# A four-layer graph network on one core: list packing placed beside layer 1, rows and weights loaded at other points, early groups of layer 3 taken feature by feature

## The chip, the core and the metric

The kernel runs on one core of a Trainium2 chip. The engines named below are TensorE (PE, with its weight loads as PEld), VectorE (DVE), ScalarE (ACT), GpSimd (POOL) and SyncE (SP), which only issues DMAs. The metric is the device time of one execution in microseconds (us), less being better. The kernel before takes 2413.58 us, the median of three runs.

## The reference, cut to what matters

The input is `x` with 2708 rows of 512 features and a 0/1 adjacency matrix `adj` of 2708 x 2708 (symmetric, about 16 neighbours a row), all in float32. Four layers follow each other, each of the form `x = layernorm(x + layer(x))`:

```python
deg = maximum((adj != 0).sum(-1), 1)
# layer 0: relu((((adj + I) / deg[:, None]) @ x + x) @ W + b)
# layer 1: (dis[:, None] * adj * dis[None, :]) @ x @ W.T + b,   dis = deg**-0.5
# layer 2: two attention layers, each
proj = x @ W                       # 512 x 1024
Wh, Ws = split(proj, 2)
a = softmax(Wh @ Ws.T) * adj       # the softmax is over all 2708 columns
x = leaky_relu(a @ Wh + x)
# layer 3: adj @ (x @ W) + b
```

## The kernel before, in words

**Tiles.** Rows come in 22 blocks of 128, columns in six chunks (`CH`: four of 512, then 384 and 276), row blocks in six groups (`GROUPS`: 4, 4, 4, 4, 3, 3). Most tiles in SBUF are pages (128 x 512 float32) of one pool of 82; the 8 banks of PSUM are two halves of four. Every engine's instructions run in the order in which the program issues them: the class `Ordered` chains each one to the one before it on its engine. That helper is line 70, and so every instruction of the profile has line 70; the names of the tiles tell them apart.

**Layers 0, 1 and 3** (`Fast.step`) go chunk by chunk, and in a chunk group by group. `multiply` adds `x` (as a high and a low part, `xh` and `xl`) times the mask columns `m` to four accumulators `acc`, one for each 128 features. After the last group of a chunk `evict` copies them to `ht`; the product with the weights (`mm`), the residual and the layernorm of the chunk (`ends`) follow during the groups of the next chunk, with `run.phase` counting them.

**Lists.** An attention layer needs of each row only its neighbours. `index(k)`, a generator, works out for chunk `k` of layer 1 where each row's neighbours stand. It alternates DVE steps (`up`, `keep`, `place`, `at_row`, `hit`, `both`, `sums`) with PE steps (`rank`, `rest`, `list`); the result is `givers`. `work(engine)` runs the next step of the oldest list if it is that engine's. Before, `step` calls it for PE in phases 1 and 5 and for DVE when the phase becomes 4 and 6; what is left over runs inside the attention, called by `beat` in the projections and score loop, and `packed(k - 1)` forces what is due.

**Attention** (`Attention.layer`) takes a chunk of columns at a time. For block `j` of 22, PE forms scores `sp`, ACT copies them to `s`, and DVE keeps the greatest (`top`). PE transposes the greatest (`tr_top`, `tr_mx`). While the next chunk's scores run, `soften` takes the exponents of this chunk's (`s<-s`, DVE and ACT), sums them, multiplies by the mask, and SP stores them into a table `pairs` in DRAM, beside the rows of `Wh`. After a chunk's last store POOL gathers from it (`g`, indirect DMAs by `givers`, at most 10 ahead), and `weigh` multiplies what was gathered into `acc`. `end` adds the row of x (`xr`) and, in the second layer, the layer's input (`x1`); both are loaded on SP's queue when a block's first `weigh` is issued. `advance`, `later` and `until` are a planner's clock by estimated costs, which sets when `weigh` and `end` are called.

**Ends of the attention layers.** In the last chunk the generator `fill` gives PE other work. For the first attention layer it is `second`: it loads `wt`, `w` and `xt`, mixes the second layer's weights (`mix`) and projects. For the second layer it is `early`: it runs the first four row groups of layer 3 for the first three chunks (`TWO`), so that part of layer 3 lies beside the end of the attention; after group 3 of a chunk, ACT copies its four accumulators to pages `begun`, and `evict` adds them later. The first `next(fill)`, which issues the loads, comes once, after the 14th of the 22 score blocks of the last chunk:

```python
if n == 13 and k + 1 == len(chunks):
    next(fill)
```

Of the kernel before, what the change touches and what calls it, by code (L numbers as in the profile page):

```python
# [24 lines left out]
DC = D // P  # L25
BANK = 512

CH = [(0, 512), (512, 512), (1024, 512), (1536, 512), (2048, 384), (2432, 276)]

GROUPS = [(0, 4), (4, 8), (8, 12), (12, 16), (16, 19), (19, 22)]  # L30
# [442 lines left out]
def blocks_of(k):  # L473

    c0, cw = CH[k]
    return [(c0 // P + q, q * P, min(P, cw - q * P)) for q in range(-(-cw // P))]
# [10 lines left out]
def cost(columns):  # L487

    return 4 * columns / 2400
# [24 lines left out]
class Fast:  # L514
# [83 lines left out]
    def early(self, run):  # L598

        seq = run.seq  # L600
        self.load(*seq[0])
        self.load(*seq[1])
        yield True
        self.prepare(*seq[0])
        for t in range(4 * TWO):
            ly, k, g = seq[t]
            if t < 2:
                self.attention.need(GROUPS[t + 2][1] - 1)
            self.load(*seq[t + 2])
            if t == 4:  # L610
                self.load_weights(ly)
            if t == 4 * TWO - 1:
                self.attention.need(GROUPS[4][1] - 1)
                for j in range(*GROUPS[4]):
                    ly.rows[j] = self.attention.made[j]
            self.prepare(*seq[t + 1])
            for j in range(*GROUPS[g]):
                self.multiply(ly, k, g, [j])
                self.attention.advance(2 * cost(CH[k][1]))
                yield True  # L620
            if g == 3:
                ly.begun[k] = [self.page(f"begun{k}_{d}") for d in range(DC)]
                for d, t in enumerate(ly.begun[k]):
                    self.nc.scalar.copy(t[:, : CH[k][1]], ly.acc[k][d][:, : CH[k][1]])


    def layernorm(self, rows):
# [72 lines left out]
    def load_rows(self, ly, j):  # L700
        if ly.rows[j] is None:
            ly.rows[j] = self.page(f"x{ly.number}_{j}")
            self.nc.gpsimd.dma_start(ly.rows[j], ly.source[j])

    def halve(self, ly, j):

# [103 lines left out]
            self.k.masks[k][:, b0 : b0 + len(ats), :], at_b[:, : len(ats), :cw]  # L810
        )

    def multiply(self, ly, k, g, only=None):
        nc, cw = self.nc, CH[k][1]
        blocks = only or range(*GROUPS[g])
        two = ly.number == 3 and k < TWO
        starts, stops = ((0, 16), (15, NB - 1)) if two else ((0,), (NB - 1,))
        if blocks[0] in starts:

            half = 0 if two and blocks[0] == 0 else k  # L820
            ly.acc[k] = [self.bank(half, f"acc{ly.number}_{k}_{d}") for d in range(DC)]
        ms = ly.done["m", k, g]
        todo = [(d, j) for d in range(DC) for j in blocks]
        if k == 0 and g + 1 < len(GROUPS):
            todo.sort(key=lambda a: a[1])
        for d, j in todo:
            for x, first in ((ly.hi, True), (ly.lo, False)):
                nc.tensor.matmul(
                    ly.acc[k][d][:, :cw],
                    x[j][:, bass.ts(d, P)],  # L830
                    ms[j - GROUPS[g][0]][:, :cw],
                    start=(j in starts and first),
                    stop=(j in stops and not first),
                )
# [158 lines left out]
    def step(self, run, t):  # L993

        ly, k, g = run.seq[t]
        self.other = (k + 1) % 2
        self.before_products(run, t)
        if ly.number == 0 and (k, g) == (1, 0):
            self.attention.blank()
        if ly.number == 1 and k == len(CH) - 1 and g in (2, 3, 4):  # L1000
            self.attention.begin(g - 2)
        self.multiply(ly, k, g)
        if run.before and run.phase in (1, 5):
            self.work("PE")
        if run.before:
            self.ends(run, run.phase)
            run.phase += 1
            if run.phase in (4, 6):
                self.work("DVE")
        if g == (4 if ly.number == 3 and k < TWO else 3):  # L1010
            self.residual(ly, k)
            if k == len(CH) - 1 and ly is not run.layers[-1]:
                self.load_weights(run.layers[1])
        if g == len(GROUPS) - 1:
            if ly.number == 3:
                self.biased(ly, k)
            if ly.number == 0:
                self.degrees(ly, k, g)
            while run.before and run.phase < 2:
                self.ends(run, run.phase)  # L1020
                run.phase += 1
            self.evict(ly, k)
            run.before, run.phase = (ly, k), 0
            if ly.number == 1:
                self.jobs.append((k, self.index(k)))

    def ends(self, run, g):

# [173 lines left out]
class Chunk:  # L1202


    def __init__(self, ly, k):
        self.ly, self.k, self.cw = ly, k, CH[k][1]
        self.name = f"{ly.number}_{k}"
        self.blocks = blocks_of(k)
        self.s, self.masks, self.ends = {}, {}, []
        self.softened = 0  # L1210
        self.fetched, self.rden = [], None

        self.to_weigh = []
        for q, (i, _, _) in enumerate(self.blocks):
            ts = lists_of(i)
            self.to_weigh += [(q, t, t is ts[0], t is ts[-1]) for t in ts]
        self.to_fetch = [(q, t) for q, ts, _, _ in self.to_weigh for t in ts]
        self.first_fetch = self.to_fetch[0]
# [8 lines left out]
class Attention:  # L1227
# [93 lines left out]

    def project(self, ly, k):
        for _ in self.project_steps(ly, k):
            pass

    def project_steps(self, ly, k):

# [186 lines left out]
    def fetch(self, ch):  # L1514


        q, t = ch.to_fetch.pop(0)
        g = self.f.wide(f"g{ch.name}_{q}_{t}")
        i = ch.blocks[q][0]
        self.nc.gpsimd.indirect_dma_start(  # L1520
            out=g,
            out_offset=None,
            in_=ch.ly.pairs[ch.k % 2].rearrange("r j d -> (r j) d"),
            in_offset=bass.IndirectOffsetOnAxis(ap=self.k.givers[:, i, t : t + 1], axis=0),
            element_offset=(q // 2) * NP * (D + 2 * P) + (q % 2) * P,
        )

        begin = max(self.fetch_free, self.clock + (16 if (q, t) == ch.first_fetch else 0))
        self.fetch_free = begin + 1.15
        ch.fetched.append((g, self.fetch_free + 6))  # L1530
# [20 lines left out]
    def weigh(self, wait=False):  # L1551

        nc = self.nc
        self.fetch_ahead()
        ch = next((c for c in self.chunks if c.to_weigh), None)
        if ch is None:
            return False
        q, ts, first, last = ch.to_weigh[0]
        if len(ch.fetched) < len(ts):
            return False  # L1560
        if ch.fetched[len(ts) - 1][1] > self.clock and not wait:
            return False
        ch.to_weigh.pop(0)
        if ch.rden is None:
            self.divisor(ch)
        i, _, w = ch.blocks[q]
        gs = [ch.fetched.pop(0)[0] for _ in ts]
        if first:
            ch.acc = self.bank(1, f"acc{ch.name}_{q}")
            ch.x = self.page(f"xr{ch.name}_{q}")  # L1570
            given = self.k.saved[1] if ch.ly.number == 0 else self.k.between
            nc.sync.dma_start(ch.x[:w], given[i][:w])
            if ch.ly.number == 1:
                ch.first = self.page(f"x1{ch.name}_{q}")
                nc.sync.dma_start(ch.first[:w], self.k.saved[1][i][:w])
        c = (q % 2) * D
        for h, g in enumerate(gs):
            lo, m = (0, w) if len(gs) == 1 else (h * QW, QW)
            nc.tensor.matmul(
                ch.acc[lo : lo + m],  # L1580
                g[:, c + lo : c + lo + m],
                g[:, P - (q % 2) * P : P - (q % 2) * P + D],
                start=first,
                stop=last,
            )
        self.advance(cost(D) if len(gs) == 1 else 1.1)
        if last:
            before = getattr(ch, "first", None)
            self.later(1.5, lambda a=(ch, q, ch.acc, ch.x, before): self.end(*a))
        self.fetch_ahead()  # L1590
        return True

# [45 lines left out]
    def layer(self, ly, chunks, fill):  # L1638
        f = self.f
        self.chunks, self.made = chunks, {}  # L1640
        for k, ch in enumerate(chunks):
# [3 lines left out]
            for n, j in enumerate(js):  # L1645
# [12 lines left out]
                    f.packed(k - 1)  # L1658
                if n == 4 and k + 1 < len(chunks):
                    self.load_moving(chunks[k + 1])  # L1660
                if n == 13 and k + 1 == len(chunks):
                    next(fill)
                if old and n == 0:
                    self.greatest(old, js[-1])
# [43 lines left out]
    def second(self, first):  # L1708

        ly = self.layers[1]  # L1710
        mixing = self.mix(1)
        next(mixing)
        self.load_w(ly)
        self.load_xt(ly, 0)
        yield True
        yield from mixing
# [73 lines left out]
```

## Time and profile before

| | |
|---|---|
| three runs | 2408.57 to 2414.01 us, median 2413.58 us |
| the profiled execution | 2413.0 us, its span 2411.3 us |
| mean granted TensorE clock | 0.982 |
| layer 0, 0 to 360 us | PE busy 342.8, DVE 319.9 |
| layer 1, 360 to 618 | PE 257.9, DVE 158.9 |
| first attention projections, 618 to 781 | PE 161.6, DVE 66.8 |
| scores, first attention layer, 781 to 1296 | PE 494.1, DVE 377.4 |
| mix and projections, 1296 to 1527 | PE 218.5, DVE 57.5 |
| scores, second attention layer, 1527 to 2027 | PE 487.7, DVE 341.7 |
| end of attention with early layer 3, 2027 to 2190 | PE 139.6, DVE 71.0 |
| rest of layer 3, 2190 to 2411 | PE 203.5, DVE 82.0 |

The stages overlap at their edges; the times are cut where most of the work changes. A stage's length less PE's busy time is what PE idles there. A busy PE may also run at half clock, which shows in the granted clock. The lines of the profile give, for a group of instructions, the engine, the operation, the tile written and the tiles read (`out<-in`), and in brackets the idle time before it with the engine and tile that ended it.

### The profile page before, as it was taken

What the parts mean: (1) busy time and instruction counts of PE and PEld (TensorE: products, weight loads), DVE (VectorE), ACT (ScalarE), POOL (GpSimd) and SP (SyncE); (2) the same over time, 40 slices, a digit from 0 to 9 for tenths busy, and PEclk for the clock granted to TensorE, in tenths of its full rate; (3) what the DMA queues carried; (4) which work ended last, traced back from release to release, by engine and by line L of the source; (5) the groups of instructions that cost most, each with busy time, mean ns of one, the idle gap of its engine ahead of it and who ended that gap; (6) DMA issues with size and microseconds to landing.
All of it is one profiled execution on the core that took longest, in us unless ns stands there. A gap on an engine that the chain in (4) does not pass through costs nothing.

```text
span 2411.3 us, 26147 instructions
## 1 busy us (share of the span) xinstructions
PE 2305.6 (96%) x8518; PEld 1322.7 (55%) x8518; DVE 1475.1 (61%) x2842; ACT 653.8 (27%) x1300; POOL 770.3 (32%) x895
## 2 busy tenths in 40 slices
PE   8999999999999998999998999999999998899997
PEld 6677777777545443443554444444443454566685
DVE  7989984756535688757665511247868785623513
ACT  6444352321110122222222210123223233421121
POOL 6545541111000001634556450001643657451000
PEclk9999999999999999999999999999999998899999
DMA  9755552223454114868889895314967889872311
GB/s 349 253 182 165 175 174 77 77 75 110 150 189 181 47 53 126 297 224 284 269 292 353 269 387 207 130 40 154 325 215 270 307 273 345 247 251 93 115 54 41
DMA packets 311126, 471.74 MB, mean 196 GB/s; under 512 B 59874, under 2 KB 189418, under 8 KB 310980
## 3 DMA queue, kind: packets, MB, share of 16 engines
q1 hardware_dynamic: 249684, 236.61, 29.9%
q0 software_dynamic: 61296, 233.37, 28.0%
q8 instruction: 69, 1.13, 0.2%
q14 instruction: 77, 0.63, 0.1%
HBM read 316.01 MB, written 153.85 MB: 195 GB/s over the span
## 4 chain that ended last, share of the span: by engine, by line
PE 80%; DVE 10%; issue 3%; DMA 3%; ACT 1%; POOL 1%; SPq 1%; another core or an unknown queue 1%; DVEq 0%; ACTq 0%; POOLq 0%
PE acc L70 30%; PE sp L70 26%; PE mm L70 9%; PE wst L70 6%; PE z L70 6%; DVE s L70 2%; DVE sum L70 1%; SPq L70 1%; DMA pairs<-s 1%; DVE top L70 1%; DMA at<-in_adj_t 1%; DVE at_row L70 1%; DMA xt<-t 1%; DVE st L70 1%
## 5 line engine op out<-in xcount | busy, mean ns | idle before, releaser
L70 POOL DMA_INDIRECT g<-pairs,givers x510 | 516.3, 1012 | 955.5 <-issue 624.5
L70 PE MATMUL sp<-xs,wst_sb 128*128 128x512 f32 (+3 forms) x2112 | 805.2, 547 | 0.0
L70 PE MATMUL acc<-m,xh 128*128 128x512 f32 (+2 forms) x1584 | 588.7, 378 | 27.5 <-ACT begun L70 14.0
L70 PEld LDWEIGHTS sp<-xs,wst_sb 128*128 128x128 f32 (+1 forms) x2112 | 382.1, 187 | 403.4 <-issue 338.3
L70 PE MATMUL acc<-m,xl 128*128 128x512 f32 (+2 forms) x1584 | 574.5, 368 | 4.1 <-DVE xl L70 3.3
L70 PEld LDWEIGHTS acc<-m,xh 128*128 128x128 f32 x1584 | 301.7, 190 | 89.2 <-ACT begun L70 16.1
L70 PEld LDWEIGHTS acc<-m,xl 128*128 128x128 f32 x1584 | 302.2, 191 | 52.4 <-issue 6.2
L70 PE MATMUL acc<-g 128*32 128x512 f32 (+1 forms) x1020 | 265.2, 610 | 10.0 <-DMA g<-pairs,givers 7.9
L70 ACT COPY s<-sp 128x512 f32<-128x512 f32 (+2 forms) x252 | 132.8, 529 | 469.2 <-PE sp L70 311.2
L70 DVE TENSOR_TENSOR top<-top,s 128x512 f32<-128x512 f32 (+5 forms) x240 | 149.5, 623 | 161.2 <-ACT s L70 112.4
L70 PE MATMUL mm<-w,ht 128*128 128x512 f32 (+1 forms) x528 | 226.1, 600 | 7.7 <-DVE ht L70 7.7
L70 ACT ACTIVATE s<-s 128x512 f32<-128x512 f32 (+3 forms) x264 | 150.4, 580 | 294.4 <-DVE s L70 204.7
L70 ACT CAST m<-at 128x512 fp32r<-128x512 uint8 (+5 forms) x396 | 199.1, 567 | 68.0 <-DMA at<-mask 42.3
L70 DVE TENSOR_TENSOR sum<-sum,s 128x512 f32<-128x512 f32 (+4 forms) x252 | 156.8, 622 | 39.4 <-issue 20.9
L70 DVE TENSOR_TENSOR s<-s,a 128x512 f32<-128x512 f32 (+3 forms) x264 | 165.9, 628 | 9.1
L70 DVE TENSOR_TENSOR s<-s,shift 128x512 f32<-128x512 f32 (+3 forms) x264 | 162.8, 620 | 10.3 <-ACT shift L70 10.3
L70 PEld LDWEIGHTS mm<-w,ht 128*128 128x128 f32 (+1 forms) x528 | 96.9, 188 | 126.6 <-issue 112.3
L70 PEld LDWEIGHTS acc<-g 128*32 128x32 f32 (+1 forms) x1020 | 77.1, 136 | 147.4 <-issue 125.0
L70 PE MATMUL wst<-xt,mixed 128*128 128x512 f32 (+2 forms) x384 | 150.5, 545 | 1.7 <-issue 1.7
L70 PE MATMUL z<-w,xt 128*128 128x512 f32 (+1 forms) x352 | 150.2, 595 | 0.0
L70 DVE COPY z_sb<-z 128x512 f32<-128x512 f32 (+1 forms) x44 | 30.3, 690 | 175.8 <-PE z L70 130.8
L70 POOL DMA_DIRECT2D x<-o x44 | 25.9, 595 | 349.8 <-DVE o L70 346.1
(159 smaller groups left out, 1662.0 us busy)
## 6 DMA issues: line engine op xcount, KB each, us to landing
pairs<-s SPq DMA_DIRECT2D x378, 128.0 KB
pairs<-z_sb SPq DMA_DIRECT2D x84, 512.0 KB
at<-in_adj_t SPq DMA_DIRECT2D x88, 256.0 KB
xres<-x POOLq DMA_DIRECT2D x44, 256.0 KB
x<-o POOLq DMA_DIRECT2D x43, 256.0 KB
x<-x POOLq DMA_DIRECT2D x35, 256.0 KB
at<-mask SPq DMA_DIRECT2D x32, 256.0 KB
xt<-t SPq DMA_DIRECT2D x32, 256.0 KB
```

What stands on the lines that cost most here:

```text
L70: ins = call(*args, **kw)
```

## The change

Four things are done, and they touch separate places.

1. **List packing.** In layer 1, PE steps are taken in phases 1, 3, 4 and 5, and DVE steps when the phase becomes 3, 4 and 5, and right after a chunk's last group, when its list is appended. The first two attention projections call `beat` too.
2. **Rows of x.** `fetch` issues the load of `xr` (and `x1`) with a block's first gather; `weigh` no longer does.
3. **Loads at the attention's ends.** `fill` is advanced after the 6th, 12th and 20th score block of the last chunk. For the first attention layer these are `wt`, then `w`, then `xt`; for the second layer nothing, then masks and rows of x for layer 3, then the preparation (`xh`, `xl`, `m`) of the first group. Layer 3's rows go to SP's queue.
4. **Early groups.** From the second early group on, `multiply` is called with one feature at a time over the group's blocks, where it took one block at a time over the features; in group 3 the copy to `begun` follows each feature.

```diff
@@ -598,10 +598,12 @@
         seq = run.seq
+        yield True
         self.load(*seq[0])
         self.load(*seq[1])
         yield True
         self.prepare(*seq[0])
+        yield True
         for t in range(4 * TWO):
             ly, k, g = seq[t]
@@ -614,14 +616,19 @@
                     ly.rows[j] = self.attention.made[j]
             self.prepare(*seq[t + 1])
-            for j in range(*GROUPS[g]):
-                self.multiply(ly, k, g, [j])
+            if g == 3:
+                ly.begun[k] = []
+            for n, j in enumerate(range(*GROUPS[g])):
+                if t == 0:
+                    self.multiply(ly, k, g, [j])
+                else:
+                    self.multiply(ly, k, g, ds=[n])
                 self.attention.advance(2 * cost(CH[k][1]))
+                if g == 3:
+                    b = self.page(f"begun{k}_{n}")
+                    self.nc.scalar.copy(b[:, : CH[k][1]], ly.acc[k][n][:, : CH[k][1]])
+                    ly.begun[k].append(b)
                 yield True
-            if g == 3:
-                ly.begun[k] = [self.page(f"begun{k}_{d}") for d in range(DC)]
-                for d, t in enumerate(ly.begun[k]):
-                    self.nc.scalar.copy(t[:, : CH[k][1]], ly.acc[k][d][:, : CH[k][1]])
@@ -700,7 +707,8 @@
         if ly.rows[j] is None:
             ly.rows[j] = self.page(f"x{ly.number}_{j}")
-            self.nc.gpsimd.dma_start(ly.rows[j], ly.source[j])
+            queue = self.nc.sync if ly.number == 3 else self.nc.gpsimd
+            queue.dma_start(ly.rows[j], ly.source[j])
     def halve(self, ly, j):
@@ -810,17 +818,17 @@
         )
-    def multiply(self, ly, k, g, only=None):
+    def multiply(self, ly, k, g, only=None, ds=range(DC)):
         nc, cw = self.nc, CH[k][1]
         blocks = only or range(*GROUPS[g])
         two = ly.number == 3 and k < TWO
         starts, stops = ((0, 16), (15, NB - 1)) if two else ((0,), (NB - 1,))
-        if blocks[0] in starts:
+        if blocks[0] in starts and 0 in ds:
             half = 0 if two and blocks[0] == 0 else k
             ly.acc[k] = [self.bank(half, f"acc{ly.number}_{k}_{d}") for d in range(DC)]
         ms = ly.done["m", k, g]
-        todo = [(d, j) for d in range(DC) for j in blocks]
+        todo = [(d, j) for d in ds for j in blocks]
         if k == 0 and g + 1 < len(GROUPS):
             todo.sort(key=lambda a: a[1])
@@ -1000,12 +1008,12 @@
             self.attention.begin(g - 2)
         self.multiply(ly, k, g)
-        if run.before and run.phase in (1, 5):
+        if run.before and run.phase in (1, 3, 4, 5):
             self.work("PE")
         if run.before:
             self.ends(run, run.phase)
             run.phase += 1
-            if run.phase in (4, 6):
+            if run.phase in (3, 4, 5):
                 self.work("DVE")
         if g == (4 if ly.number == 3 and k < TWO else 3):
@@ -1023,6 +1031,7 @@
             if ly.number == 1:
                 self.jobs.append((k, self.index(k)))
+                self.work("DVE")
     def ends(self, run, g):
@@ -1209,6 +1218,7 @@
         self.softened = 0
         self.fetched, self.rden = [], None
+        self.x, self.first = {}, {}
         self.to_weigh = []
@@ -1321,7 +1331,7 @@
     def project(self, ly, k):
         for _ in self.project_steps(ly, k):
-            pass
+            self.f.beat()
     def project_steps(self, ly, k):
@@ -1516,7 +1526,14 @@
         q, t = ch.to_fetch.pop(0)
         g = self.f.wide(f"g{ch.name}_{q}_{t}")
-        i = ch.blocks[q][0]
+        i, _, w = ch.blocks[q]
+        if q not in ch.x:
+            ch.x[q] = self.page(f"xr{ch.name}_{q}")
+            given = self.k.saved[1] if ch.ly.number == 0 else self.k.between
+            self.nc.sync.dma_start(ch.x[q][:w], given[i][:w])
+            if ch.ly.number == 1:
+                ch.first[q] = self.page(f"x1{ch.name}_{q}")
+                self.nc.sync.dma_start(ch.first[q][:w], self.k.saved[1][i][:w])
         self.nc.gpsimd.indirect_dma_start(
             out=g,
@@ -1563,16 +1580,10 @@
         if ch.rden is None:
             self.divisor(ch)
-        i, _, w = ch.blocks[q]
+        w = ch.blocks[q][2]
         gs = [ch.fetched.pop(0)[0] for _ in ts]
         if first:
             ch.acc = self.bank(1, f"acc{ch.name}_{q}")
-            ch.x = self.page(f"xr{ch.name}_{q}")
-            given = self.k.saved[1] if ch.ly.number == 0 else self.k.between
-            nc.sync.dma_start(ch.x[:w], given[i][:w])
-            if ch.ly.number == 1:
-                ch.first = self.page(f"x1{ch.name}_{q}")
-                nc.sync.dma_start(ch.first[:w], self.k.saved[1][i][:w])
         c = (q % 2) * D
         for h, g in enumerate(gs):
@@ -1585,8 +1596,8 @@
         self.advance(cost(D) if len(gs) == 1 else 1.1)
         if last:
-            before = getattr(ch, "first", None)
-            self.later(1.5, lambda a=(ch, q, ch.acc, ch.x, before): self.end(*a))
+            a = (ch, q, ch.acc, ch.x.pop(q), ch.first.pop(q, None))
+            self.later(1.5, lambda: self.end(*a))
         self.fetch_ahead()
         return True
@@ -1658,7 +1669,7 @@
                 if n == 4 and k + 1 < len(chunks):
                     self.load_moving(chunks[k + 1])
-                if n == 13 and k + 1 == len(chunks):
+                if n in (5, 11, 19) and k + 1 == len(chunks):
                     next(fill)
                 if old and n == 0:
@@ -1710,7 +1721,9 @@
         mixing = self.mix(1)
         next(mixing)
+        yield True
         self.load_w(ly)
+        yield True
         self.load_xt(ly, 0)
         yield True
```

## The prediction

> **What bounds the kernel now.** I read the page first, then TensorE's waits, then windows of the stages around the waits, and last the timelines of the engines that release them. The page:
>
> ```profile
> PE 2305.6 (96%) x8518; PEld 1322.7 (55%) x8518; DVE 1475.1 (61%) x2842; ACT 653.8 (27%) x1300; POOL 770.3 (32%) x895
> ```
>
> TensorE sets the time. The change removes no matmul, so it can gain only what TensorE idles, plus the half clock after idling. Its waits, with total, times and longest in us:
>
> ```profile
> PE acc L70 <- ACT begun L70: 14.0, 3, 6.6
> PE list L70 <- DVE both L70: 11.5, 4, 7.3
> PE tr_top L70 <- DVE top L70: 8.9, 1, 8.9
> PE acc L70 <- ACT m L70: 8.6, 5, 3.7
> PE acc L70 <- DMA g<-pairs,givers: 7.9, 2, 6.4
> ```
>
> Their places are in the TensorE timeline (start, length, operation, idle time before it; two more begun waits, 3.25 and 4.11, stand before 2139.88 and 2190.46):
>
> ```profile
> 930.65 0.74 PE L70 MATMUL list<-both,at_row 128*128 128x24 bf16 x22 [7.35 <-DVE both L70]
> ...
> 1322.89 0.88 PE L70 MATMUL tr_top<-ident,top 128*128 128x128 f32 x3 [8.89 <-DVE top L70]
> ...
> 2014.57 3.67 PE L70 MATMUL acc<-g 128*128 128x512 f32 x4 [6.44 <-DMA g<-pairs,givers]
> ...
> 2090.29 0.80 PE L70 MATMUL acc<-m,xh 128*128 128x512 f32 x1 [6.60 <-ACT begun L70]
> ```
>
> Windows (length; busy us of PE, PEld, DVE, ACT, POOL; granted clock; DMA share; GB/s) show the cover in layer 1, its lack in the scores, a restart at half clock, and a full DMA:
>
> ```profile
> 420.00:480.00 60.00, 60.00 (x266) 44.14 (x265) 40.26 (x76) 17.45 (x35) 6.61 (x12) 1.00 0.24 78
> ...
> 900.00:960.00 60.00, 49.82 (x174) 22.57 (x173) 55.65 (x109) 16.25 (x29) 7.20 (x7) 0.91 0.36 112
> ...
> 2090.00:2096.00 6.00, 5.71 (x13) 4.48 (x14) 3.30 (x9) 4.39 (x10) 1.41 (x2) 0.50 1.03 345
> ```
>
> Work at clock c costs (1 - c) of its busy time: 2.9 us in the last row.
>
> **Packing moved beside layer 1.** In the scores DVE is busy 55.65 of 60 us, and a list step is a wait for TensorE:
>
> ```profile
> 926.36 3.22 DVE L70 TENSOR_TENSOR at_row<-upto,row 128x1024 bf16<-128x1024 bf16 x3
> ...
> 930.17 0.43 DVE L70 TENSOR_TENSOR both<-hit,block 128x264 bf16<-128x264 bf16 x1
> ```
>
> With hit (0.42) and the first half of both (0.29) between them that is 4.4 us a step, 6.7 where the place arithmetic precedes it (924.0 to 930.6). By the program order all packing now ends in the second attention projection, ahead of all scores. Six waits go: 1.36 (742.9), 2.59 (796.2), 1.88 (896.9), 2.63 (909.5), 7.35 (922.7), and 1.57 for mx at 963.8, where DVE was late: 17.4. The half clock after two of them goes too: 1.1 (clocks 0.79 and 0.93 from 796 to 808) + 2.7 (0.50 from 930 to 936) = 3.8, together 21.2.
>
> Against that, layer 1 gets about two more DVE steps, 9 to 11 us, in each chunk of some 57 us, and twice the PE work slots. DVE is busy 40 of 60 there, so on average they lie beside the products. In detail a step must finish while one group multiplies: three blocks x 4 features x 2 halves x 0.227 us = 5.45 us at 512 columns, scaled 4.1 at 384, 2.9 at 276. DVE needs 4.4 to 6.7, and between two steps about 2 us for the next group's feeds reduction (3.95 for two at 452.1). I expect residual waits of 1.3 in the chunk with the first place step, 2 to 3 in chunk 4, 2 to 4 in chunk 5, and nothing in the others: 5.5, bounds 1 to 16 (three times that, if DVE lags). Net 16, bounds 5 to 20. The extra beats in the projections have a slot of 12 or more matmuls and cost nothing; if not, at most the 1.36 seen there. The matmuls waiting behind a late list are the next group's, and the evictions behind those.
>
> **Rows of x with the first fetch; loads in three parts, first attention layer's end.** tr_top's 8.89 us is put down to DVE top, but DVE itself stood 15.56 us on the DMA of xr, queued ahead of that top. SP shows why:
>
> ```profile
> 1285.67 6.54 SPq L70 DMA_DIRECT2D wt<-in_w_t  x8
> ...
> 1301.92 11.61 SPq L70 DMA_DIRECT2D pairs<-s  x8
> 1314.18 0.32 SPq L70 DMA_DIRECT2D xr<-x  x1
> ```
>
> Eight loads of wt, four of w and four of xt, issued at once, put the queue behind, and xr stood after eight stores. In the new order that xr stands six blocks of stores earlier, behind only 12 of the loads, 8 of which go out about 28 us sooner, beside the stores of 1257, when the DMA share is 0.46 (1254 to 1260). Behind those eight stand the pair stores of the chunk, 6.5 us later for it; its gathers wait for the last store alone, which SP, with nothing queued between 1245 and 1256, can reach in time. It should land by 1300 against a need at 1308. Gain: 8.89, plus half clock 1.6 + 1.2 (0.50 and 0.79 in the two windows from 1320) = 11.7. The next block's xr still follows the last pair store; the share is 1.0 from 1278 to 1320, so gathers that now have 9 us of grace may be late. I take 10; bounds 3 and 13 (the 1.43 gather wait at 1299.3 goes too). The other 43 xr move across pair stores at 0.3 to 0.9 us an issue, hidden by the 10 fetches ahead; uncovered, that is the same 0.9 us per block, below 1 us on TensorE each.
>
> **Second attention layer's end.** POOL issued eight rows of x between gathers, 4.4 us of issuing, 7.0 between two gathers:
>
> ```profile
> 2000.31 3.30 POOL L70 DMA_DIRECT2D x<-x  x6
> ...
> 2007.28 0.99 POOL L70 DMA_INDIRECT g<-pairs,givers  x1 [1.13 <-DMA x<-x]
> ```
>
> That gather landed 6 us on, and TensorE waited 6.44. All 16 rows move to SP. If gathers follow each other every 1.3 us, 6.44 goes, with half clock 1.8 (clock 0.67, 5.43 busy us from 2014 to 2020): 8. The next wait, 3.71 on m and 1.73 on xl at 2029 to 2035 with 2.6 of clock (0.75 and 0.68 from 2032), is early work that now is prepared before the last scores: of 8 I take 3, since ACT and DVE do it in the same stretch, and ACT's copies of the last two score tiles now stand behind it: rows of x that land late would hold the score banks and TensorE for as long. Against: SP is behind, and the DMA is full (share 1.05 from 2014). Rows x3_12 to 15 wait on SP for stores landing at 2059 to 2061, ahead of 66 pair stores at 0.6 us: those gathers come 2 to 4.5 us later, hidden by POOL's own 13 us idle before them at 2150.9; without that cover, 4.5 on TensorE. Net 11, bounds 0 and 16. A rule of the Trainium skill speaks against this part: "DMA: Bandwidth & Descriptors", section "Issuing engines are not separate DMA queues", says all issuers share 16 engines, so another issuer saves only issue time. By that rule this first term would be about 4.4 of issuing and not 8; the share of 1.05 agrees, the 7.0 us gap says POOL's order counts too.
>
> **Early groups by features.** Before, the four features end together, then ACT copies four accumulators while TensorE waits. Now feature 0 is copied during feature 1, so the three waits, 6.60 + 3.25 + 4.11 = 13.96, lose their cause; half clock 2.9 + 1.4 (0.91 and 0.81 from 2136) + 2.3 (0.55 and 0.88 from 2188) goes with them: 20.6. What is next late: for begun0 ACT, in step with DVE on the exps at 1.2 us each, now three blocks sooner, 2.5 (0 to 5); for begun1 the copy stays behind the layernorm's square root (2134.7), 1; for begun2, whose copies were behind such a root,
>
> ```profile
> 2189.68 0.20 ACT L70 ACTIVATE rs_t<-rs_v 128x3 f32<-128x3 f32 x1 [37.53 <-DVE rs_v L70]
> 2189.82 2.06 ACT L70 COPY begun<-acc 128x512 f32<-128x512 f32 x4
> ```
>
> the copies now precede it, 0.7; and a group needs all four m and xl before its first feature, 1.7 more at 2068, where 3.35 is lost to m already. Residue 5.9, and 0.7 of clock: net 14, bounds 6 and 20.
>
> **Sum.** 16 + 10 + 11 + 14 = 51, from the profiled execution's 2413.0 (span 2411.3; median of the runs 2413.58, 0.6 away): 2362.
>
> **Rivals.** First, waits move on more than they vanish: lower bounds 5 + 3 + 0 + 6 = 14, midway to the sum about 30, time 2383 to 2399. For it: full DMA at both ends, ACT and DVE in lockstep at 2080. Against: three of the four places have a named queue that is really reordered. Second, slower: DVE cannot follow in layer 1. There are some 20 slots; a step wholly in the open costs 4.4 us, 88 in all, so with the other 35 us gained the time is 2413 - 35 + 88 - 21 of old waits gone = 2445. It decides from a mean of (35 + 21 + 7) / 20 = 3.2 us a slot; for it the 2.9 us groups of chunk 5, against it 20 idle us of DVE in every 60. Third, the change doesn't do what it says: the early copies still wait for ACT and xr for the full DMA, packing trades even, 2413.
>
> **Chances.** Forecast 0.64, first rival 0.23, third 0.05, second 0.08. The measurement can tell 0.3%, 7 us. Faster takes the forecast and the first rival less 0.01: 0.86; same 0.06; slower 0.08. The forecast's own bounds reach 5 + 3 + 0 + 6 to 20 + 13 + 16 + 20 = 69 gained, 2344; the range goes from 2345 to 2396, most of the first rival.
>
> **What would show it.** No list or rest wait after 781; DVE under 45 of 60 at 900 to 960; list waits under 6 us in total in layer 1; no xr wait near 1314 and the clock at 1.00 there; gathers without x rows between them at 2000; begun waits below 5 us together; TensorE still busy near 2305 less the half-clock time. List waits above 3 us each in layer 1, or a begun wait of old size, would prove me wrong.

## The result and the profile after

The changed kernel takes 2392.76 us against 2413.8 us for the kernel before, both medians of four runs: a ratio of 0.9914 (95% interval 0.9901 to 0.9927). It is faster, by 21 us, where 51 were forecast. The time lies inside the stated range, but where the first rival had it (2383 to 2399) and not at the forecast of 2362. The profiled execution took 2390.8 us (span 2388.9), 22.2 less than the one of before.

The page of the changed kernel, and some of its TensorE waits (total, times, longest, us):

```profile
PE 2305.8 (97%) x8518; PEld 1315.5 (55%) x8518; DVE 1476.1 (62%) x2842; ACT 655.3 (27%) x1300; POOL 761.0 (32%) x879
```

```profile
PE list L70 <- DVE both L70: 9.2, 5, 3.8
PE mm L70 <- DVE ht L70: 7.5, 4, 2.6
PE tr_mx L70 <- DVE wide L70: 5.8, 7, 3.7
...
PE acc L70 <- DVE sums L70: 3.8, 2, 2.7
...
PE wst L70 <- issue: 3.5, 1, 3.5
...
PE acc L70 <- ACT begun L70: 2.7, 1, 2.7
```

TensorE does the same work. The waits on begun (14.0 before), tr_top (8.9) and gathers (7.9) have shrunk or gone; those on lists stand at 9.2 after 11.5, and a wait on sums is new. To see where time came and went I took the start of the same TensorE instruction in both traces:

| instruction | before, us | after, us | after less before |
|---|---|---|---|
| a product mm of layer 1's chunk 4 | 590.87 | 605.13 | +14.3 |
| a z of the second projection | 697.70 | 726.56 | +28.9 |
| first tr_top of the scores | 869.64 | 889.04 | +19.4 |
| tr_top of the scores' third chunk | 1065.03 | 1063.84 | -1.2 |
| a wst after the mix | 1357.23 | 1351.90 | -5.3 |
| tr_top, fifth chunk, second attention layer | 1961.97 | 1957.18 | -4.8 |
| tr_mx behind it | 1963.82 | 1961.97 | -1.9 |
| first mm of layer 3 | 2219.84 | 2197.29 | -22.6 |
| last products of layer 3 | 2395.17 | 2372.75 | -22.4 |

Before any changed step the changed kernel is 1.1 us ahead. So the packing brought nothing, the first attention layer's end 4, and the stretch from the second layer's end through the early groups 17, net of 3 lost at 1962.

The packing's 29 us in layer 1 and the projections are 11 list products of 0.7 us that merely moved there, and waits. They read thus in the TensorE timeline (idle time in brackets), in DVE's around one of them, and in windows (length; busy PE, PEld, DVE, ACT, POOL; clock; DMA share; GB/s):

```profile
586.99 0.71 PE L70 MATMUL list<-both,at_row 128*128 128x24 bf16 x22 [2.54 <-DVE both L70]
...
598.92 0.39 PE L70 MATMUL acc<-m,xh 128*128 128x276 f32 x1 [2.69 <-DVE sums L70]
...
690.21 0.72 PE L70 MATMUL list<-both,at_row 128*128 128x24 bf16 x22 [3.78 <-DVE both L70]
```

```profile
594.55 3.22 DVE L70 TENSOR_TENSOR at_row<-upto,row 128x1024 bf16<-128x1024 bf16 x3
597.69 0.42 DVE L70 TENSOR_TENSOR hit<-upto,which 128x264 bf16<-128x264 bf16 x1
...
598.35 0.43 DVE L70 TENSOR_TENSOR both<-hit,block 128x264 bf16<-128x264 bf16 x1
598.69 0.18 DVE L70 COPY sums<-list 128x24 f32<-128x24 f32 x1
```

```profile
580.00:640.00 60.00, 51.28 (x360) 41.21 (x360) 48.33 (x123) 9.78 (x28) 5.57 (x10) 0.95 0.43 144
640.00:700.00 60.00, 56.22 (x215) 25.14 (x214) 34.75 (x75) 4.68 (x9) 1.82 (x3) 0.97 0.21 80
900.00:960.00 60.00, 60.00 (x141) 26.57 (x140) 48.28 (x77) 20.59 (x36) 9.54 (x10) 1.00 0.57 177
```

In the scores TensorE is now full where it was busy 49.82 of 60; it pays in layer 1's last chunks, though DVE still has 12 idle us in 60 there. These do not lie where the steps need them; from 582 to 600 DVE is busy 17.8 us of 18:

```profile
582.00:588.00 6.00, 3.46 (x40) 3.15 (x39) 5.86 (x11) 0.00 (x0) 0.00 (x0) 1.00 0.13 27
588.00:594.00 6.00, 5.59 (x53) 5.28 (x53) 5.96 (x11) 3.49 (x10) 0.00 (x0) 1.00 0.11 24
594.00:600.00 6.00, 3.31 (x25) 3.09 (x25) 5.96 (x11) 0.05 (x1) 0.00 (x0) 0.97 0.08 18
```

The DVE timeline above shows a cause that the prediction did not have: a list's sums are copied out of PSUM only behind the next block's whole one-hot, and the next chunk's accumulators wait for that bank.

### The profile page after: what moved, and what is told of

Its sections match the earlier page's. It is cut to its first block, busy times and chain, and to the rows that moved or that the text cites. A ratio compares the mean times of both kernels' runs of the same rounds, so it can differ in the third digit from the quotient of the medians.

```text
span 2388.9 us, 26130 instructions
## 1 busy us (share of the span) xinstructions
PE 2305.8 (97%) x8518; PEld 1315.5 (55%) x8518; DVE 1476.1 (62%) x2842; ACT 655.3 (27%) x1300; POOL 761.0 (32%) x879
## 4 chain that ended last, share of the span: by engine, by line
PE 83%; DVE 7%; issue 4%; DMA 3%; POOL 2%; ACT 1%; SPq 0%; another core or an unknown queue 0%; DVEq 0%; POOLq 0%; ACTq 0%
PE sp L70 30%; PE acc L70 30%; PE mm L70 9%; PE z L70 6%; PE wst L70 6%; POOL g L70 1%; DVE at_row L70 1%; DMA g<-pairs,givers 1%; DVE rs_t L70 1%; DMA at<-in_adj_t 1%; DVE feeds L70 0%; DVE st L70 0%; PE tr_x2b L70 0%; PE tr_x2t L70 0%; PE list L70 0%
## 5 line engine op out<-in xcount | busy, mean ns | idle before, releaser
L70 PE MATMUL wst<-xt,mixed 128*128 128x512 f32 (+2 forms) x384 | 157.2, 563 | 3.5 <-issue 3.5
## 6 DMA issues: line engine op xcount, KB each, us to landing
at<-in_adj_t SPq DMA_DIRECT2D x88, 256.0 KB
xres<-x POOLq DMA_DIRECT2D x44, 256.0 KB
x<-o POOLq DMA_DIRECT2D x43, 256.0 KB
x<-x SPq DMA_DIRECT2D x37, 256.0 KB
at<-mask SPq DMA_DIRECT2D x32, 256.0 KB
xt<-t SPq DMA_DIRECT2D x32, 256.0 KB
```

The lines of the kernel that those rows point to most:

```text
L70: ins = call(*args, **kw)
```

## The experiments

Executions of one kernel in one set of runs lie 3 to 16 us apart (n_all: 2364.42 to 2380.27), and sets on different chips differ by 1.2%: the kernel before took 2413 to 2415 us in three sets and 2385 to 2386 in two, called the faster chips below. Kernels are therefore compared by their ratio to the kernel before on their own chip; the changed kernel's is 0.9914 on the first and 0.9903 on another. A trace shows one execution, so a wait that differs by a few us between two traces need not come from the edit. The expectations were written in us of the first kind of chip.

**Packing as before, the rest as changed** (u_pack):

```diff
-        if run.before and run.phase in (1, 3, 4, 5):
+        if run.before and run.phase in (1, 5):
-            if run.phase in (3, 4, 5):
+            if run.phase in (4, 6):
-                self.work("DVE")          # after the chunk's end
-            self.f.beat()                 # in project
+            pass
```

> The changed kernel with the packing calls as before (the other three parts kept). The prediction's term (packing beside layer 1 nets 16 us): 2409 us against 2393 for the changed kernel, with the six list, rest, rank and mx waits back between 742 and 966. Theory that the move is a wash (21 us of waits and half clock saved in the scores, 20 paid again in layer 1 and the projections): 2392 to 2394, with TensorE's waits on lists gone between 400 and 690.

2393.49 us, ratio 0.9916 (0.9895 to 0.9937): no difference from the changed kernel. The move is a wash, as the second theory had it. The waits of before are back in their old places:

```profile
PE list L70 <- DVE both L70: 11.6, 4, 7.3
```

**Sums before the next one-hot** (n_sums), and **looser slots** (n_all, with it): three steps a chunk with two groups of products each, and in a beat the DVE step right behind the PE step:

```diff
+            if ps is not None:                      # n_sums
+                nc.vector.tensor_copy(sums[:, q - 1, :], ps)
             if q < n:
                 rows, both = self.one_hot(...)
-            if ps is not None:
-                nc.vector.tensor_copy(sums[:, q - 1, :], ps)
...
-        if self.beats % 3 != 1:                     # n_all
-            self.work(("DVE", "", "PE")[self.beats % 3])
+        if self.beats % 3 == 2:
+            self.work("PE")
+            self.work("DVE")
...
-        if run.before and run.phase in (1, 3, 4, 5):
+        if run.before and run.phase in (1, 3, 5):
-            if run.phase in (3, 4, 5):
+            if run.phase in (2, 4):
```

> The changed kernel with a list step's copy of the sums ahead of the next one-hot instead of behind it. Theory that the bank of the list's sums, held for a whole one-hot, keeps the next chunk's accumulators waiting (1.07 and 2.69 us at 431 and 599): these two waits go, 2388 to 2390 us. Rival (DVE is simply late there, the wait moves to the next list or to ht): 2392 to 2394.

> The changed kernel with PE steps in phases 1, 3 and 5 and DVE steps when the phase becomes 2 and 4 and after a chunk's end (three steps with two groups of products each, in place of four of which three have one group), the copy of the sums first, and in a beat the DVE step right behind the PE step. Theory that the steps' slots are too short and nothing else: 15 of the 20 us come back, 2375 to 2379, no list wait above 1.5 us before 780. Rival that DVE has no room beside layer 1 at all: 2388 to 2394, with the same waits at other places.

n_sums: 2385.4 us, 0.9878 (0.9856 to 0.99), on u_pack's chip; both waits on sums are gone, and the trace is 4.5 us ahead of the changed kernel's by the first tr_top of the scores. By time it gains 9 us on the changed kernel, more than was expected and more than its trace, of the slowest of its four executions, shows. n_all: 2374.85 us there, 0.9833 (0.9796 to 0.987); the same instruction comes 21.4 us sooner than in the changed kernel. Its windows over the same time as above, with no list or sums wait left among TensorE's first ten:

```profile
580.00:640.00 60.00, 59.31 (x372) 43.26 (x371) 43.44 (x107) 11.69 (x31) 5.54 (x10) 1.00 0.39 134
640.00:700.00 60.00, 60.00 (x206) 27.21 (x203) 39.24 (x98) 5.06 (x11) 3.97 (x7) 1.00 0.48 177
...
900.00:960.00 60.00, 59.74 (x163) 26.43 (x161) 43.46 (x70) 17.73 (x31) 17.19 (x18) 1.00 0.57 179
```

DVE has the room; the changed kernel's slots were too short. The gain that was forecast for packing is there, in other slots. The order of the copy has 4.5 us of it by the traces and 9 by time; the phases and the beats were not undone singly.

**Rows with the first weigh again** (u_rows) and **loads at once again, at both ends** (u_three: one advance of `fill` after the 14th block, the added yields taken out; SP keeps layer 3's rows):

> The changed kernel with the rows of x loaded with a block's first weigh again. The prediction's step (the xr loads' place in SP's queue is most of the gain at the first attention layer's end): about 10 us lost, 2400 to 2403, DVE waiting on xr near 1310. Rival (the loads in three parts do it alone, the rows' place hardly counts): 2391 to 2394. A second rival: rows held longer keep pages busy, and the 3.66 us wait of tr_mx near 1958 goes with them: 2389 to 2391.

> The changed kernel with all loads at an attention layer's end issued at once after the 14th score block again. The prediction's step (sixteen loads at once put SP behind, and that holds xr): tr_top waits 6 to 9 us again near 1310, 2398 to 2403 us. Rival (the rows' earlier place does it alone): 2391 to 2394. A third view (the DMA is full from 1264 to 1336 whatever the order, so the wait only changes its place between tr_top and wst): the sum of idle and half clock between 1290 and 1345 stays within 3 us, 2391 to 2396.

u_rows: 2393.52 us, 0.9916 (0.9894 to 0.9939), no difference. u_three: 2372.12 us, 0.9949 (0.9931 to 0.9968), 8 to 11 us more than the changed kernel would take on that chip (0.9903 to 0.9914). In neither does tr_top wait near 1310, so u_three's time is as its first theory had it without that theory's sign. wst waits 5.2 and 5.3 us instead, but that is no sign of the edits: traces with the changed kernel's loads at that place have this wait between 1.8 and 8.5 (n_sums 1.8, u_x3 2.3, the changed kernel 3.5, u_feat 4.8, u_pack 5.2, r_after 8.5). Nor does u_three's loss show at the first layer's end: from a tr_top at 1243 to a wst at 1343 it takes 100.3 us, as u_feat does on the same chip with the loads in parts there. So I undid both at the first layer's end alone (u_both), and the loads in parts at the second layer's end alone (u_end2):

> The changed kernel with the rows of x loaded with the first weigh and the first attention layer's loads at once after the 14th block (both undone there; the second layer's end as changed). Each undone alone brought no tr_top wait back. If either suffices to keep xr in time, both undone bring it back: tr_top waits 6 to 11 us near 1310 on DVE and xr, the following wst wait falls below 2, and the time is 4 to 9 us above the changed kernel, ratio to the kernel before 0.993 to 0.995. Rival (the full DMA sets the end of that stretch whatever waits first): ratio 0.990 to 0.992.

> The changed kernel with the second attention layer's loads for layer 3 at once after the 14th block and the first early preparation after them, as before; the first layer's end as changed. Loads at once at both ends gave 0.9949. If that cost lies at the second layer's end (m and xl late for the first early groups): 0.994 to 0.996. If it lies at the first one: 0.990 to 0.992. The prediction gave this piece 3 us and the first end most of 10.

u_both: 2397.25 us, 0.9929 (0.9908 to 0.9949), which by itself is not clear of the changed kernel's time; but the wait is back, in TensorE's list and in DVE's timeline:

```profile
PE tr_top L70 <- DVE top L70: 14.9, 2, 13.2
```

```profile
1325.59 0.75 DVE L70 SCALAR_TENSOR_TENSOR xr<-acc,rden,xr 128x512 f32<-128x512 f32 x1 [19.76 <-DMA xr<-x]
```

SP issues that row only at 1322.61, behind w, xt and eight stores. Either step alone keeps xr in time; the second adds nothing that these runs can tell. u_end2 took 2393.95 us, 0.9923 (0.9899 to 0.9947): 2 to 5 us, too few for its interval to part the two views by time. Between the traces of these two, made on one chip, the first layer's end differs by 7.0 us (a wst at 1353.41 against 1361.64, 8.2 apart, after 1.2 at the scores before it). u_end2's own trace loses 6.9 us to the changed kernel's between 1957 and 2027 (its tr_top there is 8.0 late, after 1.1), and gets 3.4 of it back by the last products.

**Layer 3's rows on POOL again** (u_x3) and **the early groups block by block with the copies together** (u_feat):

```diff
-            queue = self.nc.sync if ly.number == 3 else self.nc.gpsimd       # u_x3
-            queue.dma_start(ly.rows[j], ly.source[j])
+            self.nc.gpsimd.dma_start(ly.rows[j], ly.source[j])
...
-                if t == 0:                                                   # u_feat
-                    self.multiply(ly, k, g, [j])
-                else:
-                    self.multiply(ly, k, g, ds=[n])
+                self.multiply(ly, k, g, [j])
```

> The changed kernel with layer 3's rows on POOL's queue again. The prediction's step (eight issues of rows between gathers cost TensorE 6.44 us and its half clock): a gather wait of 5 us or more near 2005, 2399 to 2401 us. Rival by the skill's rule on one set of DMA engines (only 4.4 us of issuing is saved): 2396 to 2398. Second rival (the full DMA alone sets when gathers land, and the wait went with the earlier time of the loads): 2391 to 2394.

> The changed kernel with the early groups block by block and the four copies together after group 3. The prediction's step (14 us, of them 20.6 gained and 6.6 paid): 2405 to 2409 us, three begun waits of 3 to 7 us. Rival (the copies' wait is partly cover for DMA and for m and xl, which come next): 2398 to 2402, with m or gather waits shorter by what begun waits are longer.

u_x3: 2370.05 us, 0.994 (0.9922 to 0.9959), 6 to 9 us above the changed kernel's ratio; TensorE waits for gathers again, 4.8 us in all, though none of these waits is above 2.8. u_feat: 2372.91 us, 0.9946 (0.9925 to 0.9967), 8 to 10 us; two of the three waits on begun are there, the one that stood at 2136 is not:

```profile
PE acc L70 <- DMA g<-pairs,givers: 4.8, 3, 2.8
```

```profile
PE acc L70 <- ACT begun L70: 12.2, 2, 8.2
```

The kernel before has just these two on a faster chip (r_before, below), so the third wait, 3.25 us in the first trace, can be absent without the other parts of the change:

```profile
PE acc L70 <- ACT begun L70: 12.2, 2, 8.1
```

u_feat's ratio is the one that its rival had (2398 to 2402 us of the first kind of chip). The rival's sign is not there: TensorE's waits on m and on gathers together are 6.2 us in u_feat and 7.2 in r_after, not less by what the begun waits are more.

**What stays at the first layer's end.** After the mix, wst waits for ACT's copies of mixed, and those for exponents that DVE feeds. I loaded all rows of a chunk with its first gather, on top of n_all, first on another chip than n_all (n_rows), then both on one chip (r_all, r_rows) with the kernel before (r_before) and the changed kernel (r_after):

> The kernel with the looser packing (2375), and all rows xr of a chunk of the first attention layer loaded with the chunk's first gather, some 40 us sooner for its last block. Theory that at the first layer's end DVE waits for the last row of x, which takes 25 us to land in a full DMA, and ACT's copies of mixed and TensorE's wst wait behind that: DVE's 6.6 us wait at xr and the 6.2 us wait of wst near 1310 fall below 2, 2368 to 2371 us. Rival (the mixed copies are late for the exponents before them, or the DMA holds something else up): 2373 to 2377.

> The changed kernel on the same chip. If its gain does not depend on the chip: 0.991 of the kernel before (21 us). If part of the gain lies in stretches where the DMA is full, and the chip where the kernel before is faster has a faster DMA, the gain there is smaller in these stretches and the ratio above 0.993; the packing's move nets within 2 us on any chip.

> The looser packing on the same chip: 0.983 of the kernel before, 17 to 19 us below the changed kernel, all of it ahead of 781 us of the changed kernel's trace. The rival (its 2375 was the chip's spread of runs) would have it within 6 us of the changed kernel.

> All rows xr of a chunk with its first gather, on top of the looser packing, on the same chip. Theory (a row that takes 20 us or more to land holds DVE, the mixed copies and wst at the first attention layer's end): 4 to 7 us below the looser packing, the wst wait below 2 us. Rival (the last run's lower wait was the chip's faster DMA): within 2 us of the looser packing, wst wait as there.

n_rows: 2342.45 us, 0.9826 (0.9808 to 0.9845). On the one chip: r_before 2385.0 us, 0.9998; r_after 2364.99, 0.9903 (0.9882 to 0.9923); r_all 2348.99, 0.9847 (0.9829 to 0.9864); r_rows 2343.61, 0.9816 (0.9799 to 0.9833). As a whole the changed kernel's gain is the same on this chip as on the first within the intervals, and the slots gain on both (16 us here, some 20 by the ratios on u_pack's chip). The gain's parts are not the same: from the tr_mx at 1962 to the first mm of layer 3 the changed kernel's trace is 20.7 us shorter than that of before on the first chip (256.0 to 235.3) and 10.3 on this one (238.2 to 227.9). r_after's trace is of the slowest of its four executions (2359.05 to 2372.85), so where the rest lies here is not shown.

wst's wait is 8.5 us in r_after, 3.5 in r_all, which has the same loads at that place, and in r_rows

```profile
PE wst L70 <- ACT mixed L70: 1.7, 1, 1.7
```

as before the change (1.7). By time r_rows is 5.4 us below r_all, but the two intervals overlap a little, and n_rows (0.9826) is no better than n_all (0.9833). The theory behind it has no support in these traces: near that place DVE waits for no row in any of the three (r_after, r_all, r_rows), but for the masks, 9.3, 4.2 and 2.3 us. So I loaded the masks sooner (n_mask, ahead of xt after the 20th block):

> Looser packing, all rows xr with a chunk's first gather, and the masks of the last chunk of the first attention layer loaded two blocks before that layer's scores end, ahead of xt. In the last two traces DVE waited 4.2 and 2.3 us on those masks, with the copies of mixed and wst behind. If the masks' place on SP's queue holds it: wst wait below 0.5, 1 to 4 us off, ratio 0.979 to 0.981. If xt or the gathers then land late instead: 0.981 to 0.983.

2369.95 us, 0.9822 (0.9796 to 0.9847): no gain over r_rows, and wst waits 5.1 us on this chip, one of the slower. The masks' place is not what holds it. DVE waits for no row and no mask there. It idles 11.4 us before a top at 1292.87, for which the trace names no cause, and 5.4 before xr at 1310.27, which needs the last matmuls of its accumulator, and these need gathers. The timeline has those matmuls end by 1306.89, but their semaphore updates come at 1310.07 to 1310.37, so TensorE's busy time can hide a wait there. Whether the gathers land late stays open.

## Why the prediction was right or wrong

**Packing: 16 forecast, 0 measured; this is the step that failed.** The saving was right: the waits and half clock of 21.2 us left the scores. The term that was mis-sized is "residual waits ... 5.5, bounds 1 to 16". The trace has eight above 1 us, 1.24 + 1.07 + 2.54 + 2.69 + 1.25 + 1.85 + 3.78 + 1.20 = 15.6 us, and after three of them a stretch at clock 0.72 to 0.75, 1.5 us each, for which the sum had no term: 20.

Two of the waits were foreseen at their size: 1.24 in the chunk with the first place step (1.3 forecast) and 2.54 in chunk 4 (2 to 3). The parts named with them, 1.3, 2 to 3 and 2 to 4, add to 5.3 to 8.3, so that 5.5 is their low end. Two things were not foreseen. One is the bank held by the sums (1.07 and 2.69; shown by n_sums); the 2.69 stands in chunk 5, where 2 to 4 was forecast for its short groups, so this number came out by luck. The other is that "the extra beats in the projections ... cost nothing", at most 1.36, was wrong: they cost 1.25, 1.85, 3.78 and 1.20, 8.1 in all. DVE's steps before the first three take 4.0 to 4.4 us, the last of them behind 5 us of a layernorm, and did not fit between a beat's DVE step and its PE step (gone in n_all). The mean of 20 idle us in 60 said that the work fits; the slot between two steps of a chain, with all that stands on DVE ahead of them, says when. Of the signs that the prediction named, DVE under 45 of 60 at 900 to 960 (48.28) and no list wait after 781 (1.20 at 796) failed with it; begun waits below 5 (2.7) held.

**First attention layer's end: 10 forecast, 4 to 7 measured in traces.** The reading of the stall was right, DVE behind a row of x behind SP's loads (u_both). Two things failed. The two edits were added up as one cause though either suffices (u_rows and u_three bring no tr_top wait). And what else a full DMA holds up ("gathers ... may be late") was priced at 1.7, by taking 10 of 11.7; wst's wait, 1.73 before, became 3.5, with 2.7 more for a clock of 0.79 and 0.64 from 1330 to 1342, and 8.5 in r_after, where DVE stands 9.3 us at a mask.

**Second layer's end: 11 forecast; 6 to 9 by u_x3 for the rows' queue and 2 to 5 by u_end2 for the parts.** The terms were 8 and 3. The Trainium skill, "DMA: Bandwidth & Descriptors", section "Issuing engines are not separate DMA queues", says that another issuer saves only the time of issuing. That is 4.4 us in the trace of before, where the first term took 8. The run gives 6 to 9, but its interval (0.9922 to 0.9959) has room for 4.4 as well, so it is not shown that more than issue time was saved. The late pairs behind x3_12 to 15 show nowhere in TensorE's waits. A cost that was not foreseen is 3 us at 1962, a tr_mx wait of 3.7 us for wide. In the changed kernel it stood beside stores of x that had not landed; pages of x held longer would explain that, and u_rows, which holds fewer, hasn't got the wait there, though it has one of tr_mx, 5.8 us, at 1252; but u_both holds as few and still waits 2.9 at that place, and on the faster chips no trace has it. Its cause stays open.

**Early groups: 14 forecast, 8 to 10 by u_feat.** The residue was about right in size and not in place: begun0's wait vanished, and the last copy of the third chunk still stands behind the layernorm's root, 2.7 us where 0.7 was written:

```profile
2162.40 0.59 ACT L70 COPY begun<-acc 128x512 f32<-128x512 f32 x1 [3.36 <-PE acc L70]
2169.52 0.20 ACT L70 ACTIVATE rs_t<-rs_v 128x3 f32<-128x3 f32 x1 [6.54 <-DVE rs_v L70]
2169.63 0.57 ACT L70 COPY begun<-acc 128x512 f32<-128x512 f32 x1
```

The gain was mis-sized for the kind of chip that it was measured on: on one of the faster chips the kernel before has 12.2 us of begun waits (r_before) and not the 13.96 of the first trace, and with the 2.7 that stay 9.5 are left of them. u_feat did not run on a slower chip.

**Rivals.** The first one, waits that move more than they vanish, is what happened; it was argued from the DMA and ACT, and happened most in packing. The second, DVE without room beside layer 1, was half seen: the price in the changed kernel is about 1 us for each of its 20 slots, not 4.4, and n_all shows that the room is there. That the time lies inside the stated range is no success of the forecast: the range (2345 to 2396) took in most of the first rival.

## What to carry to other kernels

Work that is moved under another stage is not covered by that stage's mean idle share: take the chain, list for each step the time between the instruction that feeds it and the one that needs it, and what stands on its engine in between, and give a step two slots rather than one. Copy a result out of PSUM before starting the next step, not behind it. Where two edits remove the same wait, undo each alone and both together before adding up their gains; here the version with looser slots and a chunk's rows loaded at once (r_rows) is the fastest, 0.9816 of the kernel before, twice the change's own gain; the looser slots alone (r_all) have 0.9847, and the rows' share is not clear of the noise.

## What was not expected of the hardware

The same kernel differed by 1.2% between sets of runs on different chips of the same kind. The traces of the kernel before, on a slower chip and a faster one, are 0.3 us apart up to the z at 753 and 3.0 at 1245; the distance then grows by 5 at the first attention layer's end (wst at 1357.23 and 1349.31), and from 11 at 1962 to 29 at the first mm of layer 3 (2219.84 and 2191.03). Both places begin with 60 us of DMA share 1.0 (1260 to 1320, 1980 to 2040); through layer 1 and the projections, with shares up to 0.5, the two stay equal. A full DMA alone does not tell the chips apart: from 1380 to 1440 the share is 1.03 and the distance does not grow.
